# Softmax denominators by 32x32 transposes and one product, in a two-layer attention kernel on one core

## The chip, the core and the metric

The kernel runs on one core of a Trainium2 chip. The core has five engines that work side by side, each with an in-order queue of its own: TensorE (PE, matrix products; PEld in the profile is its weight load), VectorE (DVE), ScalarE (ACT), GpSimd (POOL) and SyncE (SP). SP and POOL, and at the start ACT, also issue DMAs. The metric is the device time of one execution in microseconds (us); several executions give a median.

## What is computed

Two self-attention layers follow each other on 4 images of 64x64 tokens with 256 channels, all in float32. Cut to what matters:

```python
# first layer, N = 4096 tokens, queries and keys of 32 channels, values of 256
q, k, v = x @ Wq + bq, x @ Wk + bk, x @ Wv + bv
x = gamma * softmax(q @ k.T) @ v + x
# second layer, values of 128 channels, then a product back to 256
f, g, v = x @ Wf + bf, x @ Wg + bg, x @ Wh + bh
x = x + (softmax(g @ f.T) @ v) @ Wo + bo
```

## The kernel before

The function `fast_path` holds all the work here. Scores are computed transposed, keys on partitions and queries along the free axis, so the exponentials feed the next product with no transpose. No maximum is subtracted; a check at the end looks whether all sums and values stayed in range, and otherwise a general path runs (it doesn't here).

**Blocks and steps.** An image takes 16 blocks of 256 queries in the first layer (8 steps each, 4 key tiles of 128 a step) and 8 blocks of 512 queries in the second (16 steps each, 2 key tiles a step). A `Step` computes scores `st` on PE, and ACT turns them into `p` (L544). Where a step is split, for precision, ACT also makes a rounded `high` (L542), DVE makes `low = p - high` (L555) and a correction `d` (L560), and PE multiplies all three with their own parts of the values. All first-layer steps are split, and steps 0, 3, 5, 8, 11 and 13 of a second-layer block (`SPLIT1`). Other second-layer steps multiply `p` itself, in full float32 (two records on PE for each product).

**Order.** The main loop runs over all steps. In step n it writes `d` of n, `low` of n+1, the addition to the sums, the scores of n+2, then side work, then the products of n. Side work comes from `plan`: projections of the coming layer or image (`transpose_unit`, `qk_unit`, `v_unit`) and the ends of the block before, each put at a step by number. A scheduler sets the final order on each engine from this.

**Denominators.** In the first layer a column of ones in the values gives them. In the second they are summed apart: over a block, `p` of most steps is added into `p_sum` on DVE (L571, L573), and `p` of the steps in `MOVED_SUMS` is added into `p_sum_moved` (slot `e`) by DMAs issued from POOL, the first as a copy (L548), the others accumulating (L550). `end_second` adds both (L659), takes `o` from the accumulators (L657), folds the two key tiles (L660, `sums`), and returns four `output` units, put at steps 1 to 4 of the next block. Each one multiplies 128 queries of `o` with `Wo` (L667), and, to sum over partitions and turn the result, multiplies the same 128 columns of `sums` with one column of ones:

```python
nc.tensor.matmul(ps[:, C : C + 1], sums[:, tok], ones[:, :1], start=True, stop=True)   # L668
nc.vector.reciprocal(inverse[:, 1, n : n + 1], ps[:, C : C + 1])                        # L670
y = small(f"y_{key}_{t}")
nc.scalar.activation(y, ps[:, :C], AF.Copy, scale=inverse[:, 1, n : n + 1])             # L673
```

POOL then adds `y` to the output in memory by an accumulating DMA (L675).

**Buffers.** `wide` tiles are 128x1024: slots `t` (2, for `high` and for `p` of split second-layer steps), `p` (3), `l` (2), `d` (1, `d` of the first layer and `p_sum`) and `e` (1). `small` tiles are 128x256 (4 slots): `x_res` and `x1` of the first layer's ends, `y`, and `good` of the final check. `whole` in `qk_unit` has a buffer of its own.

**Queues.** SP loads `x_res` (L750) and `squares` (32x32 pieces of the input that DVE transposes into `xT`, L392), and stores `x1`, the first part of the output, and queries and keys (L446). POOL loads queries and keys back (L493), adds biases (L639, L751), and issues the moved sums.

**End.** After the last output DVE checks `inverse` and `seen_v` (L808 to L819), PE counts (L821), and all engines read the flag.

Of the kernel before, what the change touches and what calls it, by code (L numbers as in the profile page):

```python
# [57 lines left out]
P = 128  # L58
# [9 lines left out]
SPLIT1 = (0, 3, 5, 8, 11, 13)  # L68
MOVED_SUMS = (0, 4, 7, 9, 12)

# [168 lines left out]
def fast_path(ctx: ExitStack, tc: tile.TileContext, x, w0, w1, wo, bo, gamma, out, off):  # L239
# [27 lines left out]
    def wide(tag, name, dtype=F32):  # L267
        return work.tile([P, 2 * QB], dtype, tag=tag, bufs={"d": 1, "e": 1, "p": 3}.get(tag, 2), name=name)

# [39 lines left out]
    nc.vector.memset(ones, 1.0)  # L309

    inverse = const.tile([P, 2, B * N // P], F32, name="inverse")
    seen_v = const.tile([P, 2, B * NH], F32, name="seen_v")
# [11 lines left out]
    for l, (q_w, q_b, k_w, k_b, v_w, v_b) in enumerate((w0, w1)):  # L324
        queue = (nc.scalar, nc.gpsimd)[l]
        w_sb = work.tile([P, NCC, 2 * D], F32, tag="small", bufs=4, name=f"wqk_whole{l}")
        b_sb = const.tile([2 * D, 1], F32, name=f"bqk{l}")
        for g, w_dram, b_dram in ((0, q_w, q_b), (D, k_w, k_b)):
            queue.dma_start(w_sb[:, :, g : g + D], w_dram.rearrange("(c p) d -> p c d", p=P))
            queue.dma_start(b_sb[g : g + D, :], b_dram.rearrange("(d o) -> d o", o=1))  # L330
        w_parts = const.tile([P, NCC, 4 * D], F32R, name=f"wqk{l}")
        high, low = w_parts[:, :, : 2 * D], w_parts[:, :, 2 * D :]
        nc.scalar.copy(high, w_sb)
        nc.vector.tensor_sub(low, w_sb, high.bitcast(F32))
        wqk.append(w_parts)
        bqk.append(b_sb)
        v_sb = const.tile([P, NCC, CV[l]], F32, name=f"wv{l}")
        queue.dma_start(v_sb, v_w.rearrange("(c p) d -> p c d", p=P))
        wv.append(v_sb)
# [20 lines left out]
    def bias_units():  # L360


        def issue():
            nc.vector.tensor_scalar(bv, bv, gamma_sb, None, ALU.mult)
            wide_bias = work.tile([P, P], F32, tag="small", bufs=4, name="wide_bias")
            nc.vector.memset(wide_bias, 1.0)
# [8 lines left out]
    qk_dram, x1_dram = {}, {}  # L375
    q_t, moved_sums, first_p, waiting = {}, {}, [], {}

# [34 lines left out]
    def project_units(b, l, h):  # L412
# [5 lines left out]
        def qk_unit():  # L418
            ps = side_psum(f"psqk_{b}_{l}_{h}")[:, :QB0]
            for c in range(NCC):  # L420
                for n in range(2):
# [6 lines left out]
                    )  # L428
            whole = data.tile([2 * D, QB0], F32, tag="qk", name=f"qk_{b}_{l}_{h}")
            lead = b == l == 0 and h % 2 == 1  # L430
# [16 lines left out]
            halves[b, l, j] = part + 1  # L447
            if l == 0 and b > 0:
                load_half(b, h + 1)
            elif l == 1 and h == NH - 1:  # L450
                load_half(b + 1, 0)
            elif l == 1:
                load_squares((b, 1, h + 1), waiting.pop((b, h + 1)))
            if b == l == 0:
# [36 lines left out]
    def load_rows(dst, parts, which, order):  # L491
        for n, h in enumerate(order):
            nc.gpsimd.dma_start(dst[n * D : (n + 1) * D, :], parts[h, which])  # L493

# [15 lines left out]
    def small(name):  # L510
        return work.tile([P, C], F32, tag="small", bufs=4, name=name)


    class Step:
# [8 lines left out]
        def scores(self):  # L523
# [16 lines left out]
            if self.split:  # L540
                self.high = wide("t", f"high_{self.key}", F32R)
                nc.scalar.activation(self.high, s_flat, AF.Exp, bias=down)  # L542
            self.p = wide("t" if self.split and l == 1 else "p", f"p_{self.key}")
            nc.scalar.activation(self.p, s_flat, AF.Exp)  # L544
            if l == 1 and i in MOVED_SUMS:
                if i == MOVED_SUMS[0]:
                    moved_sums[b, j] = wide("e", f"p_sum_moved_{b}_{j}")
                    nc.gpsimd.dma_start(moved_sums[b, j], self.p)  # L548
                else:
                    nc.gpsimd.dma_start(moved_sums[b, j], self.p, accum_op=ALU.add)  # L550
# [12 lines left out]

        def add_up(self, p_sum):
            if self.l == 0 or self.i in MOVED_SUMS:
                return
            kept = [i for i in range(NI[1]) if i not in MOVED_SUMS]
            if self.i == kept[0]:
                first_p.append(self.p)
            elif self.i == kept[1]:  # L570
                nc.vector.tensor_add(p_sum, first_p.pop(0), self.p)  # L571
            else:
                nc.vector.tensor_add(p_sum, p_sum, self.p)  # L573

# [78 lines left out]

    def end_second(b, j, acc, p_sum, o):
        key = f"{b}_{j}"
        for h in range(QB // QB0):
            nc.vector.tensor_add(o[h][:, :QB0], o[h][:, :QB0], acc[1][:, h * QB0 : (h + 1) * QB0])  # L657
        sums = work.tile([P, QB], F32, tag="sums", bufs=1, name=f"sums_{key}")
        nc.vector.tensor_add(p_sum, p_sum, moved_sums[b, j])  # L659
        nc.vector.tensor_add(sums, p_sum[:, :QB], p_sum[:, QB:])  # L660

        def output(t):
            def issue():
# [3 lines left out]
                nc.tensor.matmul(ps[:, :C], part, wo_sb, start=True, stop=True)  # L667
                nc.tensor.matmul(ps[:, C : C + 1], sums[:, tok], ones[:, :1], start=True, stop=True)  # L668
                n = (b * N + j * QB) // P + t
                nc.vector.reciprocal(inverse[:, 1, n : n + 1], ps[:, C : C + 1])  # L670

# [6 lines left out]

        return [output(t) for t in range(NT)]

    def run(units):
        for u in units:
            u()


# [13 lines left out]
    keys = [(b, l, j) for b in range(B) for l in range(2) for j in range(NB)][NB:]  # L699
    acc, p_sum, units = None, None, {}  # L700

    def plan(b, l, j, ends):
# [20 lines left out]
        else:  # L723
            for n, u in enumerate(ends):
                put(1 + n, u)
        if b + 1 < B:
            for h in range(NH):
# [7 lines left out]
    for n, s in enumerate(steps):  # L735
        b, l, j = s.b, s.l, s.j
        if s.first:
            units = plan(b, l, j, ends)
            acc = [ps_main.tile([P, QB], F32, tag=f"acc{a}", name=f"acc{a}_{b}_{l}_{j}") for a in range(2)]
            if l == 0:  # L740
                pair = ps_main.tile([P, 2, QB], F32, tag="pair", name=f"acc_pair_{b}_{j}")
                acc += [pair[:, a, :] for a in range(2)]
            if l == 1:
                p_sum = wide("d", f"p_sum_{b}_{j}")
        if l == 0 and s.last:
# [22 lines left out]
        after.cut_low()  # L768
        s.add_up(p_sum)
        todo = units.get(s.i, [])  # L770
# [30 lines left out]
        if s.last:  # L801
            ends = end_first(b, j, acc) if l == 0 else end_second(b, j, acc, p_sum, o)
    run(ends)

    good = small("good").rearrange("p (l n) -> p l n", l=2)
    nc.vector.tensor_scalar(good, inverse, 1.0 / SUM_MAX, None, ALU.is_ge)  # L808
    nc.vector.tensor_scalar(inverse, inverse, 1.0 / SUM_MIN, None, ALU.is_le)
    nc.vector.tensor_mul(good, good, inverse)  # L810
    nc.vector.tensor_scalar(seen_v, seen_v, VALUE_MAX, None, ALU.is_le)
    size = const.tile([P, 1], F32, name="size")
    nc.vector.tensor_mul(size, gamma_sb, gamma_sb)
    nc.vector.tensor_scalar(size, size, GAMMA_MAX**2, None, ALU.is_le)
    low = const.tile([P, 1], F32, name="low")
    for seen, axes in ((good, AX.XY), (seen_v, AX.XY)):
        nc.vector.tensor_reduce(low, seen, axes, ALU.min)
        nc.vector.tensor_mul(size, size, low)
    nc.vector.tensor_scalar(low, size, 1.0, None, ALU.is_lt)  # L819
# [53 lines left out]
```

## Time and profile before

| what | value |
|---|---|
| median of 3 runs | 3159.63 us (3158.0 to 3161.63) |
| profiled execution, its own time | 3155.92 us |
| span of the profiled execution | 3154.1 us |
| busy PE / DVE / ACT / POOL | 3116.3 / 2689.1 / 2140.1 / 900.7 us |
| accumulating DMAs of the moved sums, issue to landing | 4.5 / 4.9 / 6.5 us (least, median, most) |
| longest total wait on ACT | `high` for scores on PE, 362.8 us in 358 waits |

Busy time is the time in which an engine has an instruction running; matrix products are pipelined and their ends are modelled. In a row of groups stand line, engine, operation, output and inputs with shapes, the count, then busy time and mean duration in ns, then the idle time ahead of the group and what ended it. In a timeline the first two numbers are start and duration. Names without numbers stand for all buffers of that name.

### The profile page before, as it was taken

To read this page: it belongs to the slowest core of one execution; us is meant where nothing else is said; L and a number is where in the kernel's file an instruction comes from. 1 tells how busy PE (TensorE), PEld (TensorE's weight loads), DVE (VectorE), ACT (ScalarE), POOL (GpSimd) and SP (SyncE) were. 2 spreads that over 40 slices of the span, in tenths; PEclk is the share of its full clock that TensorE was granted. 3 is DMA by queue.
4 is the path that set the end of the run, shared out by engine and by line. 5 is a ranking of instruction groups with operands and counts; after the bars stand their busy time and mean duration, and the time that the engine had idled before them with its cause. 6 is when DMAs were issued, how large, how long until landed. Compare 5 with 4: busy or idle time off the path is not lost.

```text
span 3154.1 us, 54090 instructions
## 1 busy us (share of the span) xinstructions
PE 3116.3 (99%) x19908; PEld 2672.0 (85%) x19908; DVE 2689.1 (85%) x3237; ACT 2140.1 (68%) x2835; POOL 900.7 (29%) x1108
## 2 busy tenths in 40 slices
PE   8999999999999999999999999999999999999997
PEld 7999998666799999866679999976668999996664
DVE  7888888888888888888888888898888888888876
ACT  7666666777666666777766666677776666666674
POOL 5232224222422222422242222232223222233221
PEclk9999999999999999999999999999999999999999
DMA  4121114555512121555541112255554111125454
GB/s 119 43 53 47 48 48 104 107 108 105 104 44 51 41 53 47 113 101 112 107 93 47 49 45 51 51 116 107 105 113 81 48 46 47 49 65 105 97 95 73
DMA packets 391392, 239.49 MB, mean 76 GB/s; under 512 B 266672, under 2 KB 355248, under 8 KB 391120
## 3 DMA queue, kind: packets, MB, share of 16 engines
q0 software_dynamic: 68160, 134.86, 22.0%
q1 hardware_dynamic: 322048, 100.76, 13.4%
q8 instruction: 161, 2.64, 0.4%
q14 instruction: 111, 0.91, 0.1%
q10 hardware_dynamic: 912, 0.33, 0.1%
HBM read 82.58 MB, written 67.11 MB: 47 GB/s over the span
## 4 chain that ended last, share of the span: by engine, by line
PE 91%; DVE 3%; DMA 2%; issue 2%; ACT 1%; POOL 0%; SPq 0%; DVEq 0%; ACTq 0%; POOLq 0%
PE acc L600 24%; PE acc L582 23%; PE acc_pair L582 23%; PE st L532 14%; PE psv L464 4%; PE psqk L422 2%; PE pso L667 2%; DVE d L560 1%; DVE low L555 1%; ACT p L544 1%; DVE p_sum L573 1%; DMA p_sum_moved<-p 0%; DMA squares<-in_x 0%; PE pso L668 0%; DMA squares<-x_dram 0%
## 5 line engine op out<-in xcount | busy, mean ns | idle before, releaser
L542 ACT ACTIVATE high<-st,down 128x1024 fp32r<-128x1024 f32 x704 | 786.5, 1117 | 703.2 <-PE st L532 362.8
L544 ACT ACTIVATE p<-st 128x1024 f32<-128x1024 f32 x1024 | 1042.5, 1021 | 166.3 <-PE st L532 143.8
L560 DVE SCALAR_TENSOR_TENSOR d<-low,high 128x1024 fp32r<-128x1024 f32 x704 | 871.0, 1237 | 227.0 <-PE acc_pair L582 223.7
L555 DVE TENSOR_TENSOR low<-p,high 128x1024 fp32r<-128x1024 f32 x704 | 936.6, 1330 | 142.6 <-ACT p L544 141.6
L532 PE MATMUL st<-q,k 128*128 128x256 f32 (+1 forms) x3072 | 706.3, 338 | 2.5 <-DMA k<-qk_parts 1.4
L600 PE MATMUL acc<-p,v 128*128 128x512 f32 x1280 | 611.0, 597 | 0.0
L532 PEld LDWEIGHTS st<-q,k 128*128 128x128 f32 x3072 | 470.0, 189 | 103.3 <-issue 40.6
L639 POOL TENSOR_TENSOR x_res<-x,bo 128x256 f32<-128x256 f32 x128 | 212.5, 1660 | 879.3 <-DVE x L628 879.2
L600 PEld LDWEIGHTS acc<-p,v 128*128 128x128 f32 x1280 | 233.1, 189 | 161.8 <-issue 143.4
L573 DVE TENSOR_TENSOR p_sum<-p_sum,p 128x1024 f32<-128x1024 f32 x288 | 352.6, 1224 | 9.4 <-ACT p L544 5.8
L582 PE MATMUL acc<-v0h,high 128*128 128x258 f32 x2048 | 341.6, 284 | 1.2 <-ACT high L542 1.2
L582 PE MATMUL acc<-v0d,d 128*128 128x258 f32 x2048 | 339.2, 287 | 2.6 <-DVE d L560 2.2
L582 PE MATMUL acc<-v0l,low 128*128 128x256 f32 (+1 forms) x2048 | 329.3, 283 | 0.6 <-DVE low L555 0.5
L582 PE MATMUL acc_pair<-v0h,high 128*128 128x258 f32 x2048 | 329.8, 283 | 0.0
L582 PE MATMUL acc_pair<-v0l,low 128*128 128x256 f32 (+1 forms) x2048 | 328.8, 282 | 0.0
L582 PE MATMUL acc_pair<-v0d,d 128*128 128x258 f32 x2048 | 328.5, 282 | 0.0
L582 PEld LDWEIGHTS acc<-v0h,high 128*128 128x128 f32 x2048 | 286.0, 189 | 3.1 <-issue 1.4
L582 PEld LDWEIGHTS acc<-v0d,d 128*128 128x128 f32 x2048 | 281.5, 190 | 5.6 <-DVE d L560 4.9
L582 PEld LDWEIGHTS acc<-v0l,low 128*128 128x128 f32 x2048 | 282.2, 190 | 1.8 <-DVE low L555 1.3
L582 PEld LDWEIGHTS acc_pair<-v0h,high 128*128 128x128 f32 x2048 | 282.1, 189 | 0.0
L582 PEld LDWEIGHTS acc_pair<-v0l,low 128*128 128x128 f32 x2048 | 281.1, 189 | 0.0
L582 PEld LDWEIGHTS acc_pair<-v0d,d 128*128 128x128 f32 x2048 | 281.0, 189 | 0.0
(108 smaller groups left out, 3332.5 us busy)
## 6 DMA issues: line engine op xcount, KB each, us to landing
p_sum_moved<-p POOLq DMA_DIRECT2D x160, 512.0 KB, 4.7
x_res<-in_x SPq DMA_DIRECT2D x128, 128.0 KB, 2.1
qk_dram<-qk_parts SPq DMA_DIRECT2D x128, 128.0 KB, 1.9
x_dram<-x SPq DMA_DIRECT2D x128, 128.0 KB, 1.7
out<-x_res SPq DMA_DIRECT2D x128, 128.0 KB, 1.7
squares<-x_dram SPq DMA_DIRECT2D x512, 32.0 KB, 1.9
out<-y POOLq DMA_DIRECT2D x128, 128.0 KB, 3.2
q<-qk_dram POOLq DMA_DIRECT2D x252, 64.0 KB, 2.2
```

The costliest lines, as they stand in the source:

```text
L422: nc.tensor.matmul(ps, wqk[l][:, c, :], x_parts[key][n][:, c, :], start=(c == n == 0), stop=(c == NCC - 1 and n == 1),)
L464: nc.tensor.matmul(ps[:, t, :], xT[key][:, c, t * P : (t + 1) * P], wv[l][:, c, :], start=(c == 0), stop=(c == NCC - 1),)
L532: nc.tensor.matmul(st[:, g, :], k_t[b, l, kt // NT][:, kt % NT * P : (kt % NT + 1) * P], q_t[b, l, j * n // QB][:, q0 : q0 + n], start=Tru ...
L542: nc.scalar.activation(self.high, s_flat, AF.Exp, bias=down)
L544: nc.scalar.activation(self.p, s_flat, AF.Exp)
L555: nc.vector.tensor_sub(self.low, self.p, self.high.bitcast(F32))
L560: nc.vector.scalar_tensor_tensor(self.d, self.low.bitcast(F32), -UP, self.high.bitcast(F32), ALU.mult, ALU.add)
L573: nc.vector.tensor_add(p_sum, p_sum, self.p)
L582: nc.tensor.matmul(acc[2 * s + which][:, :width], p[:, g * QB0 + s * P : g * QB0 + (s + 1) * P], v0[self.i][v][:, g, :width], start=self.f ...
L600: nc.tensor.matmul(acc[which], v_part[:, g, :], p[:, g * QB : (g + 1) * QB], start=first and g == 0, stop=last and g == G[1] - 1,)
L639: nc.gpsimd.tensor_add(x_old[s], x_new[s], bo_sb)
L667: nc.tensor.matmul(ps[:, :C], part, wo_sb, start=True, stop=True)
```

## The change

It has five parts.

1. The denominators of all second-layer blocks but the very last are computed in two new units ahead of the outputs. `turn` transposes the 512 columns of `sums` in 32x32 squares on DVE and reduces each square, which leaves 16 partial sums on each partition. `denominators` multiplies those with a constant `same` (ones where two partitions have the same number modulo 32) on PE, and four reciprocals of 32 partitions each write `inverse`. The four outputs follow at steps 3 to 6. The last block keeps the column of ones.
2. Six steps instead of five are moved sums: 3, 4, 6, 7, 9, 12. The first is split, and ACT writes its `p` straight into slot `e`, so there is no copy; the other five accumulate into it. `issue_after` puts these DMAs behind the load of queries or keys that was written last. `p_sum` is allocated at the second kept step, and `sums` lies in its first half, the transposed squares in its second.
3. Slot `t` has three buffers, `small` three, and `whole` is a `small` tile.
4. In `qk_unit` the loads of the next half block's `squares` are written ahead of the store of queries and keys.
5. The check of all earlier blocks is put at step 13 of the last block, and only the last four columns are checked at the end. `good` is a `t` tile.

```diff
-MOVED_SUMS = (0, 4, 7, 9, 12)
+MOVED_SUMS = (3, 4, 6, 7, 9, 12)
...
-        return work.tile([P, 2 * QB], dtype, tag=tag, bufs={"d": 1, "e": 1, "p": 3}.get(tag, 2), name=name)
+        return work.tile([P, 2 * QB], dtype, tag=tag, bufs={"d": 1, "e": 1, "p": 3, "t": 3}.get(tag, 2), name=name)
...
+    same = const.tile([P, P], F32, name="same")
+    nc.gpsimd.tensor_copy(same[:, :S], ident[:, :S])
+    for a in range(1, P // S):
+        nc.gpsimd.tensor_add(same[:, :S], same[:, :S], ident[:, a * S : (a + 1) * S])
+    for a in range(1, P // S):
+        nc.gpsimd.tensor_copy(same[:, a * S : (a + 1) * S], same[:, :S])
...
+            if l == 0 and b > 0:
+                load_half(b, h + 1)
+            elif l == 1 and h == NH - 1:
+                load_half(b + 1, 0)
+            elif l == 1:
+                load_squares((b, 1, h + 1), waiting.pop((b, h + 1)))
-            whole = data.tile([2 * D, QB0], F32, tag="qk", name=f"qk_{b}_{l}_{h}")
+            whole = small(f"qk_{b}_{l}_{h}")[: 2 * D, :]
...
-            nc.gpsimd.dma_start(dst[n * D : (n + 1) * D, :], parts[h, which])
+            loads[0] = nc.gpsimd.dma_start(dst[n * D : (n + 1) * D, :], parts[h, which])
...
-        return work.tile([P, C], F32, tag="small", bufs=4, name=name)
+        return work.tile([P, C], F32, tag="small", bufs=3, name=name)
...
-            self.p = wide("t" if self.split and l == 1 else "p", f"p_{self.key}")
+            base = l == 1 and i == MOVED_SUMS[0]
+            self.p = wide("e" if base else "t" if self.split and l == 1 else "p", f"p_{self.key}")
             nc.scalar.activation(self.p, s_flat, AF.Exp)
-            if l == 1 and i in MOVED_SUMS:
-                if i == MOVED_SUMS[0]:
-                    moved_sums[b, j] = wide("e", f"p_sum_moved_{b}_{j}")
-                    nc.gpsimd.dma_start(moved_sums[b, j], self.p)
-                else:
+            if base:
+                moved_sums[b, j] = self.p
+            elif l == 1 and i in MOVED_SUMS:
+                with tc.issue_after(loads[0].ins):
                     nc.gpsimd.dma_start(moved_sums[b, j], self.p, accum_op=ALU.add)
...
-        sums = work.tile([P, QB], F32, tag="sums", bufs=1, name=f"sums_{key}")
-        nc.vector.tensor_add(p_sum, p_sum, moved_sums[b, j])
-        nc.vector.tensor_add(sums, p_sum[:, :QB], p_sum[:, QB:])
+        sums, squares = p_sum[:, :QB], p_sum[:, QB:]
+        nc.vector.tensor_add(sums, sums, squares)
+        n0 = (b * N + j * QB) // P
+        end = b == B - 1 and j == NQ[1] - 1
+        part_sums = work.tile([P, QB // S], F32, tag="part_sums", bufs=1, name=f"part_sums_{key}")
+
+        def turn():
+            nc.vector.transpose(squares, sums)
+            nc.vector.tensor_reduce(part_sums, squares.rearrange("p (n k) -> p n k", k=S), AX.X, ALU.add)
+
+        def denominators():
+            ps = side_psum(f"psd_{key}")[:, : QB // S]
+            nc.tensor.matmul(ps, same, part_sums, start=True, stop=True)
+            for a in range(P // S):
+                rows = slice(a * S, (a + 1) * S)
+                of_rows = ps[rows, :].rearrange("p (t a) -> p t a", a=P // S)[:, :, a]
+                nc.vector.reciprocal(inverse[rows, 1, n0 : n0 + NT], of_rows)
...
-                nc.tensor.matmul(ps[:, C : C + 1], sums[:, tok], ones[:, :1], start=True, stop=True)
-                n = (b * N + j * QB) // P + t
-                nc.vector.reciprocal(inverse[:, 1, n : n + 1], ps[:, C : C + 1])
+                n = n0 + t
+                if end:
+                    nc.tensor.matmul(ps[:, C : C + 1], sums[:, tok], ones[:, :1], start=True, stop=True)
+                    nc.vector.reciprocal(inverse[:, 1, n : n + 1], ps[:, C : C + 1])
...
-        return [output(t) for t in range(NT)]
+        return ([] if end else [turn, denominators]) + [output(t) for t in range(NT)]
...
+        if (b, j) == (B - 1, NQ[1] - 1):
+            put(NI[1] - 3, check_all_but_last)
...
     run(ends)
-    good = small("good").rearrange("p (l n) -> p l n", l=2)
...
+    check(in_last_block)
```

## The prediction

> **What bounds the kernel now.** I read the page first, then busy time by stretches, then the timeline of single edges.
>
> ```profile
> PE 3116.3 (99%) x19908; PEld 2672.0 (85%) x19908; DVE 2689.1 (85%) x3237; ACT 2140.1 (68%) x2835; POOL 900.7 (29%) x1108
> ...
> PE 91%; DVE 3%; DMA 2%; issue 2%; ACT 1%; POOL 0%; SPq 0%; DVEq 0%; ACTq 0%; POOLq 0%
> ```
>
> TensorE (PE) holds the chain. A busy PE could still hide waits in modelled ends, so the next table asks where it is idle (columns: length, then busy time and count of PE, PEld, DVE, ACT, POOL, clock, DMA).
>
> ```profile
> core 0: us, PE busy (x) PEld busy (x) DVE busy (x) ACT busy (x) POOL busy (x), PEclk, DMA share, GB/s
> 0.00:80.00 80.00, 66.75 (x390) 56.74 (x391) 56.63 (x139) 56.49 (x115) 41.48 (x86) 1.00 0.46 119
> 80.00:160.00 80.00, 77.21 (x606) 74.34 (x605) 66.96 (x85) 51.65 (x68) 17.21 (x22) 1.00 0.17 43
> ...
> 2875.00:3134.00 259.00, 258.74 (x899) 164.59 (x897) 206.52 (x218) 174.85 (x202) 67.24 (x91) 1.00 0.50 95
> 3134.00:3154.20 20.20, 3.20 (x19) 2.59 (x18) 4.80 (x17) 1.79 (x4) 3.55 (x4) 0.70 0.24 30
> ```
>
> Of 37.8 us of idle PE (3154.1 - 3116.3), 13.3 + 2.8 lie in the first 160 us and 17.0 after 3134. About 5 us are left for the rest. So in the body an edit pays only by taking work off PE, and costs only where it makes PE wait. Buffers and earlier loads have next to nothing to win there.
>
> **What the Trainium skill says.** "TensorE: Matmul & The Clock Gate", section LDWEIGHTS, prices a weight load at its columns over 1.2 ns, 107 ns for 128; a wide product hides it, a one-column product can't. The trace agrees: a product L668 comes as two records, some 0.23 us together (below), near two bare loads. "VectorE: DVE Perf Modes", section The three transpose paths: the DVE transposes 32x32 blocks and never crosses them, which is why one product with `same` must still join the four groups of partitions; the trace has that transpose at 0.705 us. "Perfetto Trace Analysis", section Identifying the Most-Contended Engine: matmul busy share is no measure of headroom, and consistent bubbles mean missing buffers. Here the steps are regular and the bubbles absent. "DMA: Bandwidth & Descriptors", section Two DMAs through the same engine are not ordered: a dependent DMA needs the earlier one's semaphore. The trace shows POOL waiting so, 45.2 us in 13 waits of L550 for the last accumulation.
>
> **Part 1, the denominators.** Before, each of 128 outputs has a product L668. In the PE timeline:
>
> ```profile
> 2240.28 0.28 PE L668 MATMUL pso<-ones,sums 128*128 128x1 f32 x2
> 2240.42 1.96 PE L600 MATMUL acc<-p,v 128*128 128x512 f32 x4
> 2241.82 1.02 PE L532 MATMUL st<-q,k 128*128 128x512 f32 x2
> ...
> 2257.82 1.88 PE L600 MATMUL acc<-p,v 128*128 128x512 f32 x4
> 2259.13 1.03 PE L600 MATMUL acc<-d,v 128*128 128x512 f32 x2
> ```
>
> First column is the start. L668 holds PE for 0.14 us, and the group behind it then takes 1.40 us to the next start, against 1.31 without L668 ahead: 0.23 us each. 31 of 32 blocks change (the last keeps the old way): 124 x 0.23 = 28.5 us removed. Added: 31 products of 16 columns, two records each, same loads; 15 more columns are estimated at 0.01 us, so 31 x 0.24 = 7.4 us. **Net -21.1 us on PE.** All of it is on the path.
>
> VectorE (DVE), durations by form:
>
> ```profile
> L573 DVE TENSOR_TENSOR p_sum<-p_sum,p 128x1024 f32<-128x1024 f32 x288 | 352.6, 1224 | 9.4 <-ACT p L544 5.8
> L392 DVE STREAM_TRANSPOSE xT<-squares 128x512 f32<-128x512 f32 x112 | 79.0, 705 | 15.2 <-DMA squares<-in_x 6.5 <-DMA squares<-x_dram 5.1 <-issue 3.0
> L670 DVE RECIPROCAL inverse<-pso 128x1 f32<-128x1 f32 x128 | 20.5, 162 | 15.2 <-PE pso L668 14.2
> L817 DVE TENSOR_REDUCE low<-good 128x1 f32<-128x256 f32 x1 | 0.4, 420 | 0.0
> ```
>
> Removed: one 1.22 us addition per block, since six sums move instead of five. Added: a transpose of 0.70, and a reduction over 512 that I estimate at 0.69 from the 256-wide one (0.42) and the 512-wide passes (0.68 to 0.70). Four reciprocals stay four. Per block +0.17 us, 5 us over the run, under PE's work.
>
> **New waits in part 1.** The product with `same` waits for transpose and reduction. In the built order it stands behind the second whole step's product of the next block. Worked out from the edge at 2994: d done 2995.9, transpose to 2996.5, low (behind its p) to 2998.0, reduction to 2998.7; PE arrives at 2998.5. Where the reduction stands ahead of low, as in the last image, there is no wait. So 0 to 0.2 us. Queued behind it on PE are the next score product and the first output; behind the reciprocals on DVE the next d; ACT's y waits for the inverses, with all later exponentials behind it. ACT is 68% busy, which covers a wait of half a us.
>
> The second wait is for d. These lines of one edge show the cover that goes:
>
> ```profile
> 2994.57 0.59 PE L667 MATMUL pso<-wo,o 128*128 128x256 f32 x2
> 2994.66 1.22 DVE L560 SCALAR_TENSOR_TENSOR d<-low,high 128x1024 fp32r<-128x1024 f32 x1
> ...
> 2995.00 0.28 PE L668 MATMUL pso<-ones,sums 128*128 128x1 f32 x2
> 2995.14 1.96 PE L600 MATMUL acc<-p,v 128*128 128x512 f32 x4
> ...
> 2996.54 1.04 PE L600 MATMUL acc<-d,v 128*128 128x512 f32 x2
> ```
>
> d ends at 2995.88, PE takes it at 2996.54: 0.66 us to spare, just what L667 and L668 (0.43 + 0.23) occupy ahead of it. The outputs now start two steps later, so PE comes 0.66 us sooner. Edges of the first image spare 0.34 to 0.78 us in the same count, so 0 to 0.3 us is lost per edge. Both waits together: 0 to +8 us over 31 edges. I take **+3**.
>
> **Part 2, moved sums.** The copy L548 goes; p of step 3 is written straight into the slot `e`, and steps 4, 6, 7, 9, 12 accumulate. DMA count stays 160, but five of a block now queue one behind another, 4.9 us each (median of L550; 4.5 to 6.5). In the last image p of step 4 is issued 28.1 us ahead of L659, so five take 24.5 and the last lands some 3.5 us ahead (before: 3.6 to 5.5). Covered: 0. Behind these waits on POOL stand the stores of y and the next q loads. `issue_after` keeps the k and q loads ahead. DMA time may also fall or rise with accumulation in place of copy; I bound this part at -2 to +4 and take 0.
>
> **Part 3, buffers and queues.** The third `t` lets high of step 3 start when its scores are done, 1.2 us sooner at the edge above (it waited 1.58 us). PE was not waiting for it: 0, bounds -3 to 0. `small` has three slots and takes `whole` as well. Two x_res, two x1 and one `whole` share them in the first layer; SP's order now loads x_res behind the store of q and k, and x1 of the second tile comes 3.3 us after the first, whose store lands in 1.7 and whose POOL addition takes 1.7. In the second layer, y of one tile may wait for an earlier store (3.2 us). ACT would stop, not yet PE: 0 to +3, taken as 0. Loads of squares ahead of the store of queries and keys: eight DMAs move past one on SP; DVE's waits for them are 11.6 us in all, PE's share is within the 5 us above. -2 to +1, taken 0.
>
> **Part 4, start and end.** Seven small POOL instructions for `same` go between its weight loads. The nearest row is the POOL memset of 128x128, 0.20 us, so each load is 0.2 to 1.5 us later, and the ACT cast of the second layer's weights and DVE's gamma step wait for them in their queues. Against that, x_res leaves SP's first loads. -1 to +3, taken **+1**. The end:
>
> ```profile
> 3138.70 0.47 ACT L673 ACTIVATE y<-pso,inverse 128x256 f32<-128x256 f32 x1 [0.18 <-DVE inverse L670]
> 3140.65 0.29 DVE L808 TENSOR_SCALAR good<-inverse 128x256 f32<-128x256 f32 x1 [1.99 <-DMA out<-y]
> ...
> 3143.30 0.19 PE L821 MATMUL count<-low,ones 128*1 128x1 f32 x2 [4.85 <-DVE low L819]
> ```
>
> `good` waits 2.0 us for a slot of `small` that a store of y holds; it moves to `t`, and eight instructions shrink to six of four columns (2.5 to 1.2 us). POOL's last store is issued until 3140.8 and then bounds it: -2.9. The early checks sit between the last additions and push the last sums back by some 0.6. Hence -2.3, say **-2** (0 to -3.5).
>
> **Sum.** -21.1 + 3 + 1 - 2 = -19 us, 0.6%. The profiled execution took 3155.9 us around a span of 3154.1, and would give 3137. The median of the three runs lies 3.7 us above that, at 3159.6; I forecast **3140.5**.
>
> **Rivals.** *New waits take most of it.* If each of 31 edges loses 0.5 us at d and at the inverses, 15.5 instead of 3: -6.6 us, 3153. For it: the exact match of spare time and removed cover. Against: other products stand there in blocks with projections. *The chain of moved sums becomes the bound* (slower). If landings take 6.4 us, as two did in the last image, five need 32 us, 4 us beyond the add; 1.4 us of that may be covered, and in some 13 blocks with 35 us between adds 2.7 us are lost, +35 us: 3176. It decides from a mean landing of 5.6 us; the median of 4.9 speaks against it. *The edit does not do what it says*: PE hides L668 in part, say 0.14 us each. Then 17 - 5 = 12 is gained, with the other terms 3149. The longer group behind L668 speaks against it.
>
> **Chances.** Forecast 0.66, edges 0.13, partial price 0.10, chain 0.11. A measurement of this kernel tells about 0.2%, 6.3 us. Faster: forecast, partial price and a little of the edge case, 0.78; same 0.11; slower 0.11. Range 3132 (all low bounds but a few) to 3155 (the edge case).
>
> **What would show it.** L668 falls to 8 records, and the new product has 62 records, PE busy near 3095. Right waits: PE idle in the body still some 5 us; more than 15 would be the edge rival. The chain rival shows as the final p_sum addition waiting for a DMA. The prediction is wrong if PE busy falls by under 12 us, or if idle grows by as much as it falls.

## The result and the profile after

The changed kernel takes 3203.5 us (median of 4, 3198.1 to 3204.7) against 3158.8 us before (4, 3156.4 to 3161.6) in the same session. The ratio is 1.0138, 95% interval 1.012 to 1.0155: 44 us slower, where 19 us faster were forecast. Below, the effect of a run is its ratio to before, less one, times 3158.8 us.

Busy times and the chain of waits by engine, after:

```profile
PE 3123.4 (98%) x19722; PEld 2656.5 (83%) x19722; DVE 2710.0 (85%) x3272; ACT 2136.8 (67%) x2835; POOL 855.0 (27%) x1115
...
PE 74%; DVE 9%; DMA 6%; issue 6%; SPq 2%; ACT 1%; POOL 1%; DVEq 0%; ACTq 0%; POOLq 0%
```

PE has 186 records fewer, as the change says, yet its busy time rose by 7.1 us, and its share of the chain fell from 91% to 74%. DVE and DMA took the place. Busy time by stretches (columns as in the prediction's table) shows that it isn't the start:

```profile
core 0: us, PE busy (x) PEld busy (x) DVE busy (x) ACT busy (x) POOL busy (x), PEclk, DMA share, GB/s
160.00:500.00 340.00, 335.38 (x2774) 332.88 (x2772) 288.15 (x332) 219.86 (x281) 72.87 (x74) 1.00 0.19 47
500.00:900.00 400.00, 392.47 (x1754) 281.47 (x1753) 349.57 (x424) 280.65 (x387) 127.10 (x182) 1.00 0.56 105
```

The same stretches kept PE busy for 339.94 and 399.16 us before. The first of them is first layer only, which holds no denominators and no moved sums: 4.6 us of new idle time come from parts that were priced at nothing.

Since ends on PE are modelled, idle time understates this. So I priced each product at its usual distance to the next start (0.12 us for 256 or 258 columns, 0.23 for 512, 0.43 for 512 in full float32, 0.11 for a record of a one-column product) and counted what is left of each gap over 0.04 us. By this estimate PE's work falls by **20.8 us, near the forecast (21.1)**; since a record has one price in the whole count, this confirms how many records went, not what one is worth (e9 below does that). The gaps grow from some 51 to some 117 us, **about 66 us more**; with a usual distance for each pair of neighbouring products it is 70. The largest group of them stands ahead of the products that take `d`. Groups by line after; behind the bar stand busy time and mean, behind the second bar the idle time ahead of the group and what ended most of it:

```profile
L594 PE MATMUL acc<-v0d,d 128*128 128x258 f32 x2048 | 355.5, 291 | 27.0 <-DVE d L571 25.9
L594 PEld LDWEIGHTS acc<-v0d,d 128*128 128x128 f32 x2048 | 285.6, 190 | 45.0 <-DVE d L571 43.1
```

Before, these two idled 2.6 and 5.6 us. One first-layer edge after (where a block ends and the next begins), from the timeline (start, duration):

```profile
412.18 2.94 POOL L807 TENSOR_TENSOR x_res<-x_res,bv 128x256 f32<-128x256 f32 x2 [3.53 <-ACT high L551]
...
412.77 1.75 DVE L566 TENSOR_TENSOR low<-p,high 128x1024 fp32r<-128x1024 f32 x1
...
414.44 1.23 DVE L414 TENSOR_TENSOR xl<-xT,xh 128x512 fp32r<-128x512 f32 x1
...
416.12 1.21 DVE L571 SCALAR_TENSOR_TENSOR d<-low,high 128x1024 fp32r<-128x1024 f32 x1
...
417.38 0.63 PE L594 MATMUL acc<-v0d,d 128*128 128x258 f32 x3 [0.92 <-DVE d L571]
```

Two additions of `bv` on POOL (L751 before) run just while DVE has `low`, `xl`, both `o` and `d` to do with no gap. `low` takes 1.75 us instead of 1.22 and `xl` 1.23 instead of 0.69: 1.07 us lost, and PE waits 0.92 us for the `d` at the end of that queue. After has 42 waits of over 0.3 us ahead of these products, 33 us in sum. In the 7 us ahead of 41 of them DVE instructions were lengthened beside an addition of `bv`, by 31 us in sum. Before has four such waits, none of them with such an addition ahead. At the same edge before:

```profile
417.06 1.76 DVE L555 TENSOR_TENSOR low<-p,high 128x1024 fp32r<-128x1024 f32 x1
...
417.70 1.72 POOL L751 TENSOR_TENSOR x_res<-x_res,bv 128x256 f32<-128x256 f32 x1
```

POOL slowed `low` there too, but behind the edge (`x` was done at 412.6 and 415.9), where PE was not waiting. This addition is for the next block: before, an addition stands 22.7 us (median) ahead of the `x` that uses it, just behind the last edge; after, 7.6 us ahead, inside its own edge. Over the whole run `low` and `d` exceed 1.22 us by some 91 us in sum before and some 100 us after (counting excesses over 0.1 us, additions of both biases together). The amount of contention grows little; what changes most is its place. The Trainium skill, page "SBUF — State Buffer", section Who interferes with whom, describes this neighbour: a DVE instruction with two SBUF inputs contends with a GpSimd instruction that reads SBUF, over a port pair that they share. The trace agrees in kind: no `low`, `d` or `xl` is lengthened by over 0.1 us without a POOL addition beside it. A `low` that is hit mostly takes some 0.48 to 0.58 us longer (137 of 150 before).

### The profile page after: what moved, and what is told of

The parts are those of the page before. It is cut to its first block, busy times and chain, and to the rows that moved or that the text cites. A ratio compares the mean times of both kernels' runs of the same rounds, so it can differ in the third digit from the quotient of the medians.

```text
span 3201.7 us, 54037 instructions
## 1 busy us (share of the span) xinstructions
PE 3123.4 (98%) x19722; PEld 2656.5 (83%) x19722; DVE 2710.0 (85%) x3272; ACT 2136.8 (67%) x2835; POOL 855.0 (27%) x1115
## 4 chain that ended last, share of the span: by engine, by line
PE 74%; DVE 9%; DMA 6%; issue 6%; SPq 2%; ACT 1%; POOL 1%; DVEq 0%; ACTq 0%; POOLq 0%
PE acc L612 20%; PE acc_pair L594 18%; PE acc L594 17%; PE st L541 12%; PE psv L473 4%; DVE d L571 4%; DVE low L566 2%; PE psqk L430 2%; DMA x_res<-in_x 2%; DMA p<-p 2%; PE pso L697 1%; SPq L280 1%; DMA squares<-x_dram 1%; DVE xl L414 1%; DVE p_sum L585 1%
## 5 line engine op out<-in xcount | busy, mean ns | idle before, releaser
L571 DVE SCALAR_TENSOR_TENSOR d<-low,high 128x1024 fp32r<-128x1024 f32 x704 | 890.3, 1265 | 266.1 <-PE acc_pair L594 258.7
L566 DVE TENSOR_TENSOR low<-p,high 128x1024 fp32r<-128x1024 f32 x704 | 926.8, 1317 | 109.1 <-ACT p L555 107.8
L594 PE MATMUL acc<-v0d,d 128*128 128x258 f32 x2048 | 355.5, 291 | 27.0 <-DVE d L571 25.9
L585 DVE TENSOR_TENSOR p_sum<-p_sum,p 128x1024 f32<-128x1024 f32 x256 | 312.1, 1219 | 19.4 <-ACT p L555 17.0
L561 POOL DMA_DIRECT2D p<-p x160 | 143.4, 896 | 643.5 <-ACT p L555 289.0
L651 POOL TENSOR_TENSOR x_res<-x,bo 128x256 f32<-128x256 f32 x128 | 178.7, 1396 | 475.5 <-DVE x L640 306.7
```

The costliest lines, as they stand in the source:

```text
L566: nc.vector.tensor_sub(self.low, self.p, self.high.bitcast(F32))
L571: nc.vector.scalar_tensor_tensor(self.d, self.low.bitcast(F32), -UP, self.high.bitcast(F32), ALU.mult, ALU.add)
L585: nc.vector.tensor_add(p_sums[self.b, self.j], so_far, self.p)
L594: nc.tensor.matmul(acc[2 * s + which][:, :width], p[:, g * QB0 + s * P : g * QB0 + (s + 1) * P], v0[self.i][v][:, g, :width], start=self.f ...
L651: nc.gpsimd.tensor_add(x_old[s], x_new[s], bo_sb)
```

## The experiments

**Which part loses.** e4 undoes the prediction's part 3, e5 makes part 1 alone, e6 parts 2 and 4 alone.

```diff
 e4 (on after)
-... bufs={"d": 1, "e": 1, "p": 3, "t": 3}
+... bufs={"d": 1, "e": 1, "p": 3}
-            whole = small(f"qk_{b}_{l}_{h}")[: 2 * D, :]
+            whole = data.tile([2 * D, QB0], F32, tag="qk", name=f"qk_{b}_{l}_{h}")
-tag="small", bufs=3
+tag="small", bufs=4
 # and the load_half / load_squares lines back behind the store
 e5 (on before): `same` and the new end_second (`sums` in p_sum, the final p_sum addition ahead of `o`)
 e6 (on e4): the old end_second
```

> The kernel after with the whole third part undone: two high buffers, four slots in `small`, the sums in their own tile, the squares loads behind the store of queries and keys. What is left is the denominators, the moved sums and the check spread out. Theory A: 3158.8 - 21 (PE work removed) + 2 to 5 (edge waits) = 3138 to 3145 us. Rival B: the same. Rival C: still 3190 to 3205, the loss is in what is left.

e4: 1.0048 (1.0031 to 1.0065), +15 us. The gaps of the first image's first layer are nearly gone (under 0.7 us in each 79 us, some 1.5 to 3 after), but it does not reach 3140. Theory A explains only a part.

> The kernel before with the new end of a second-layer block alone (32x32 transposes, one product for all denominators, p_sum added to before o); the moved set, the buffers and the order of loads are those of before. e4 showed that without the third part the change still loses 17 us although 21 us of PE work are gone. Theory E (the new moved set is at fault: steps 1 and 2 of each second-layer block now put two p_sum additions of 1.22 us on DVE ahead of x of the last first-layer block, so x_dram, the squares, xT and the last keys come late, and at the other edges low and p come late): 3160 - 21 + 2 to 5 = 3141 to 3145 us. Theory C (the denominators' chain at the edge is at fault): 3165 to 3180.

e5: 1.0004 (0.9995 to 1.0012), +1 us: neither theory. The 21 us are saved and given back.

> e4 with the old end of a second-layer block, 124 sums products on PE again, so that the moved sums (3, 4, 6, 7, 9, 12), the base written straight into its tile, and the check spread out are what is left of the change. Theory E: the 17 us of e4 plus the 21 us of PE work, less 2 to 5 for the edge waits: 3193 to 3200 us. Theory C: 3155 to 3163, as before.

e6: 1.0056 (1.0039 to 1.0073), +18 us, where E had wanted twice that. So part 2 loses 14 us (e4 less e5) to 18 us whether part 1 is there or not, and part 1 is worth nothing either way.

**Buffers and queues.** e1 and e2 undo one or two of the three buffer changes, e3 and e15 make one or two alone, e8 undoes the order of loads, e11 leaves out POOL's additions.

```diff
 e2 (on after): "t": 3 taken out
 e1 (on e2)
-            whole = small(f"qk_{b}_{l}_{h}")[: 2 * D, :]
+            whole = data.tile([2 * D, QB0], F32, tag="qk", name=f"qk_{b}_{l}_{h}")
 e15 (on before): tag="small", bufs=4 becomes 3
 e3 (on e15)
-            whole = data.tile([2 * D, QB0], F32, tag="qk", name=f"qk_{b}_{l}_{h}")
+            whole = small(f"qk_{b}_{l}_{h}")[: 2 * D, :]
 e8 (on after): the load_half / load_squares lines behind the store
 e11 (on after)
-                nc.gpsimd.tensor_add(x_res[b, j][t], x_res[b, j][t], bv)
```

> The kernel after, with the query and key sums (`whole`) back in a tile of their own, tag qk; `small` stays at three slots, and the high tiles have two buffers again, which makes the room. Theory A (the sums in the ring of `small` put the x_res loads behind the store of queries and keys, so the bv additions on POOL run beside the busiest stretch of DVE at the block's edge, d is late, and PE waits about 1 us in each first-layer block): the loads stand again right behind the output stores, stalls on acc<-v0d,d fall from 52 us to under 20, time 3140 to 3160 us. Rival B (the squares loads ahead of the store do it): still 3195 to 3205, since that order stays. Rival C (moved sums and denominators at the edges): still 3195 to 3205. Rival D (third high buffer lets ACT run ahead of DVE): about 3140 to 3160 too, told apart by e2.

> The kernel after with two buffers for the high tiles, and nothing else undone. Theory A: no change against after, 3195 to 3210 us. Rival D (the third buffer is the harm): 3140 to 3160. If the third buffer helped after a little, as its purpose would have it: some us above after.

e1: 1.0103 (1.0087 to 1.012), +32 us; e2: 1.0206 (1.0189 to 1.0223), +65 us. The `small` tiles form a ring: they take its slots in turn, and a new one has to wait until the last user of its slot is done. The place of `whole`, the query and key sums, in this ring alone is worth 33 us here. In e1 the additions stand 22.1 us ahead of `x` again, and the gaps ahead of the first layer's `d` products fall from 52 to 16 us, as A said. Its time stays far above A's, in the range of B and C: it keeps three slots (e15 below) and the moved sums (e4). e2 also shows what was not forecast: the third `t` **gains** 22 us (65 less 43.6). With two, ACT's `high` waits 233.6 us for DVE's `low`; with three, `low` is no longer among the main releasers of its row.

> The kernel before with only this changed: `small` has three slots and the query and key sums take one of them. Theory A: the loss without the gain: 3158.8 + 40 to 65 = 3199 to 3224 us, with acc<-v0d,d waiting for DVE as in after. Rivals B, C and D: no change, 3155 to 3163.

> The kernel before with `small` at three slots, and nothing else. e3 lost 57 us with three slots and the sums of queries and keys in one of them. Theory A as refined (the ring's order does it, the slot does little): 3160 to 3175 us. If the missing slot is what costs: 3195 to 3220.

e3: 1.0174 (1.0157 to 1.0191), +55 us. e15: 1.0056 (1.0041 to 1.0072), +18 us. The suspected cost alone, in the kernel before, is larger than the whole loss of the change; two thirds of it, 37 us, are the sums in the ring. With them there the additions stand 7.4 us ahead of `x` in e3, as in after; with three slots alone 19.9 us. So the slot costs in another place: see the table under "Moved sums".

> The kernel after with one thing undone: the squares loads stand again behind the store of queries and keys. Theory A: nothing comes back, 3195 to 3212 us, since the x_res loads stay behind both. Rival B (the order of squares and store is at fault for part of it): 3180 or less.

e8: 1.0168 (1.0151 to 1.0185), +53 us, 9 above after, with intervals that just touch. The earlier loads seem to help a little; rival B falls.

> The kernel after without the addition of bv to x_res on POOL (128 instructions of about 1.4 us); the second layer gets an input without it. The loads of x_res stay late. Theory A (the additions beside DVE's busiest stretch make d late): the 52 us of stalls on acc<-v0d,d fall under 20, 3160 to 3175 us. If the late loads do the harm in another way (x late, the order of DVE): 3190 to 3205 us.

e11: 1.0006 (0.9997 to 1.0014), +2 us. **Leaving out 128 small POOL instructions, with every load as late as in after, gives back 42 us.** Groups by line of e11:

```profile
L594 PEld LDWEIGHTS acc<-v0d,d 128*128 128x128 f32 x2048 | 285.7, 190 | 10.9 <-DVE d L571 7.3
```

45.0 became 10.9. A rival would be that the additions hold up other work in POOL's queue while they wait for their loads. But the gaps of PE fall by 39 us, and 37 of these stand ahead of the products that take `d`, where the lengthened DVE instructions were seen. A load stands 12.0 us (median) ahead of its `x` in e11, 12.9 in after, 25.4 before: the lateness does no harm by itself; where POOL then runs does. No run leaves the additions out of the kernel before; there PE waits for `d` ahead of these products for only 2.2 us on its own row, so little could come back at this place.

**Moved sums.** e7 takes the early additions off DVE, e12 moves one more step in e5.

```diff
 e7 (on e4, add_up): steps 0 to 2 are not added, step 5 twice
+            if self.i <= 2:
+                return
+            so_far = self.p if self.i == kept[3] else p_sums[self.b, self.j]
 e12 (on e5)
-MOVED_SUMS = (0, 4, 7, 9, 12)
+MOVED_SUMS = (0, 1, 4, 7, 9, 12)
```

> e4 with the sums of steps 0, 1 and 2 left out (step 5 is counted twice in their place), which takes the two p_sum additions of steps 1 and 2 away from DVE in each of the 32 second-layer blocks; the five accumulating DMAs and their order on POOL stay. Theory E: the stalls at the edges of the second layer go back to a few us, 3143 to 3155 us. If the accumulating DMAs, or the order that holds them behind the loads of keys, are at fault: still 3172 to 3182.

e7: 0.997 (0.9959 to 0.9982), -10 us, 25 below e4. DVE has 78 us less to do in it (64 x 1.22), so this is an upper bound for what the two additions cost in their place. POOL, which waits for landings of the moved sums for 137.2 us in after and 45.2 before, keeps its five DMAs in e7, so they are not what costs the 25 us. What the additions hold up is seen in e4's timeline where the first layer ends:

```profile
523.53 1.22 DVE L585 TENSOR_TENSOR p_sum<-p,p 128x1024 f32<-128x1024 f32 x1
...
524.86 1.23 DVE L585 TENSOR_TENSOR p_sum<-p_sum,p 128x1024 f32<-128x1024 f32 x1
...
527.56 0.87 DVE L640 SCALAR_TENSOR_TENSOR x<-o,g,x_res 128x256 f32<-128x256 f32 x2
528.06 0.81 SPq L644 DMA_DIRECT2D x_dram<-x  x2
...
532.98 0.33 SPq L280 DMA_DIRECT2D squares<-x_dram  x1
```

Before, with step 0 moved, the first addition came behind the first `x`:

```profile
524.74 0.49 DVE L628 SCALAR_TENSOR_TENSOR x<-o,g,x_res 128x256 f32<-128x256 f32 x1
525.23 1.23 DVE L571 TENSOR_TENSOR p_sum<-p,p 128x1024 f32<-128x1024 f32 x1
```

So `x` is 2.8 us later, the store too, and `squares` 3.1 us later (529.91 before). PE then waits until 555.6 us for keys that POOL loaded late, 1.0 us, and shorter for `xh`, `xl` and `p` around it. All four images show the same. In the table, an edge is the last first-layer product of an image; the second column is the time from there to the first load of `squares` from the new `x`, the third how long PE idles from 20 us before to 80 us after, four images together:

| run | `squares` after the edge | PE idle at four edges |
|---|---|---|
| before | 8.2 to 8.5 us | 1.3 us |
| e5 (denominators alone) | 8.2 to 8.5 us | 2.4 us |
| e4 (all but part 3) | 12.0 to 12.8 us | 15.1 us |
| e6 (moved sums alone) | 11.9 to 12.3 us | 13.3 us |
| e7 (e4 without the early sums) | 7.2 to 7.5 us | 5.7 us |
| e15 (three slots alone) | 11.0 us | 10.7 us |

This is where e4 and e6 lose, and e7 gets most of it back. By the count of gaps, all of the 24 us that e4 has more than e5 stand at these edges, and 17 of the 19 us that e15 has more than before. The missing slot of e15 costs at the same edge by another way: its second `x` comes 3.6 us behind the first (1.7 before), and `squares` is loaded behind both.

> e5 with step 1 added to the moved set of before: (0, 1, 4, 7, 9, 12), with the copy into the moved tile as before. One p_sum addition fewer (1.22 us of DVE) in each second-layer block, at its start, where e7 showed such additions to cost most. Theory E: e5 less 5 to 12 us, 3151 to 3158 us. If one more accumulating DMA early in the block holds up the loads of keys behind it on POOL: 3165 to 3180 us.

e12: 1.0011 (1.0003 to 1.002), +3 us, nothing gained over e5. E's forecast fails here. `squares` comes 7.3 to 7.7 us after the edge in e12, but e5 has no loss at this edge to win back (2.4 us): a late `x` costs, and one that is earlier than before gains nothing.

**Denominators.** e9 takes the old products away, and e13, e17 and e16 put pieces of the new way in.

```diff
 e9 (on before)
-                nc.tensor.matmul(ps[:, C : C + 1], sums[:, tok], ones[:, :1], start=True, stop=True)
-                nc.vector.reciprocal(inverse[:, 1, n : n + 1], ps[:, C : C + 1])
+                nc.vector.reciprocal(inverse[:, 1, n : n + 1], sums[:, t : t + 1])
 e13 (on e9):  return [nothing, nothing] + [output(t) for t in range(NT)]
 e17 (on e13): return [turn, nothing] + [output(t) for t in range(NT)]
 e16 (on e5), in turn
-            nc.vector.transpose(squares, sums)
-            nc.vector.tensor_reduce(part_sums, ..., AX.X, ALU.add)
+            nc.vector.tensor_copy(part_sums, sums[:, : QB // S])
 e10 (on e5): turn empty, part_sums = sums[:, : QB // S]
 e14 (on e5): denominators and the first output in one unit
```

> The kernel before with the 128 one-column products (line 668) left out; the reciprocals stay, of a column of `sums` instead, so that DVE does what it did and the y are scaled wrongly. It gives what the price of these products is worth when nothing is put in their place. e5 gained nothing, although its PE work is 21 us less. Theory F (in the steps where these products stand PE is held to the pace of DVE and ACT anyway, and what it saves it waits): 3153 to 3163 us. Theory G (the saving is real, and the transposes, the reduction and the wait for the product eat it): 3161 - 29 = 3132 to 3137 us.

> e5 without the transposes and the reduction (0.7 and 0.64 us of DVE in each of 31 edges): the product takes the first 16 columns of the sums instead, so the denominators are wrong. Theory G (the added work of DVE at the edge eats the saving): 3163 less 15 to 20, 3140 to 3148 us. Theory F: 3155 to 3163, no change against e5.

e9: 0.9921 (0.9907 to 0.9934), -25 us: of the 29 us that 128 products are worth by the forecast's price, most come through. (The reciprocals no longer wait for PE either, so not all of it need be PE's time.) F falls. e10: 1.0001 (0.9993 to 1.001). It says nothing of G, since the product reads `p_sum` there and the next `p_sum` waits for it, 13 us on DVE; what e13's expectation takes from e10 does not hold.

> e9 (the kernel before without the 128 sums products, with reciprocals of a column of `sums`) with two empty units ahead of the four outputs, so that these stand at steps 3 to 6 of the next block as in the change, and no transposes, no product for the denominators. e10 showed that the transposes and the reduction are not what eats the 24 us that e9 gained. Theory H (the two units ahead move the outputs by two steps: ACT's y and PE's pso then stand at steps that already carry high and p of the split steps 3 and 5 and the projections of the next image, p and st come late): 3152 to 3162 us. Theory J (the one product, its wait and its place in the side PSUM ring cost it): 3133 to 3139, as e9.

> e13 (no sums products, outputs two steps later, 3139 us) with the transposes and the reduction on DVE at step 1, whose result nobody reads. Theory G: 3139 plus 12 to 20, 3151 to 3159 us. Theory J: 3137 to 3143 us.

> e5 with the transposes and the reduction left out, and a DVE copy of the first 16 columns of the sums into part_sums in their place, so that the denominators are wrong. e10 did the same but let the product read p_sum itself, so that the next p_sum had to wait for PE (13 us on DVE in its trace); the copy takes that wait away. Theory G (the 1.3 us of DVE at each edge eat the saving): 3163 less 12 to 20, 3143 to 3150 us. Theory J (the product, its four reciprocals and their waits do): 3157 to 3165.

> e5 with the denominators and the first output in one unit: turn at step 1, product and first output at step 2, the others at 3 to 5. Correct values. Theory H: about half of the loss comes back, 3148 to 3156 us. Theory J: 3158 to 3166, as e5, or more, since the first y now waits for the reciprocals.

e13: 0.9941 (0.9927 to 0.9955), -19 us. e17: 0.9958 (0.9945 to 0.9972), -13 us. e16: 0.9975 (0.9965 to 0.9984), -8 us. e14: 1.0007 (0.9999 to 1.0015), +2 us. None of the theories holds alone: e13 and e14 fall in J's ranges, e16 in G's, e17 between the two. Going from e9 to e5, 26 us are lost. `turn` takes 9 us of them where the product follows (e5 less e16); that is clear of the intervals. Smaller steps are not: some 6 us for the later outputs (e13 less e9) and some 5 us for `turn` without the product (e17 less e13) have intervals that overlap. The rest, 11 to 15 us, is the product (an estimated 7.4 us of its own time on PE) together with all else by which e5 differs from e13 and e17: the four reciprocals and their waits, `sums` inside p_sum, and the final p_sum addition ahead of `o`. No run parts these. One wait on the way shows in the groups by line of e5:

```profile
L680 PEld LDWEIGHTS psd<-part_sums,same 128*128 128x128 f32 x62 | 10.6, 188 | 14.6 <-DVE part_sums L675 11.0 <-issue 3.1
L680 PE MATMUL psd<-part_sums,same 128*128 128x16 f32 x62 | 9.9, 236 | 2.0 <-DVE part_sums L675 1.8
```

and of e16:

```profile
L679 PEld LDWEIGHTS psd<-part_sums,same 128*128 128x128 f32 x62 | 11.5, 188 | 2.5
```

The loads of the product idle 14.6 us, 11.0 of it until the reduction, and 2.5 us when a copy of 0.17 us stands in its place. But a load can idle while an earlier product still runs, and PE's own row idles only 2.0 us there (2.6 by the count of gaps). So this wait is a small part of the 9 us. By the count of gaps most of the difference is spread over other products: ahead of the scores 22 us in e5 against 16 in e16, of the outputs 10 against 5, of `low` 8 against 4.

**A version made of what helped.** e18 is e5 with the third `t`, the earlier loads, three `small` slots, and the sums in a tile of their own.

```diff
 e18 (on e5): "t": 3, tag="small" bufs=3, load_half / load_squares ahead of the store
-            parts = data.tile([P, QB0], F32R, tag="v1_parts" if lead else "qk_parts", ...)
+            parts = x_parts[key][1][:, 1, :]
```

> A version with right values that keeps what the runs showed to help and leaves what they showed to cost: the denominators of e5 with the moved set of before, the third high buffer (e2: worth 24 us in the kernel after) and the squares loads ahead of the store (e8: 10 us), while the sums of queries and keys have a tile of their own; the room comes from their parts, which lie in the low half of x, read by then, and from three slots in `small` (e15: costs 15 us). If the worths add up: 3163 - 24 - 10 + 15 = 3144 us, range 3135 to 3160, faster than both. If they were worth something only in the kernel after, where ACT and SP were late for other reasons: 3165 to 3180.

e18: 1.002 (1.0013 to 1.0027), +6 us. That is between the two ranges. The worths don't add up: third buffer and earlier loads repay some 13 of the 18 us that the missing slot costs, not 31 (the new place of the parts was not run alone). The second `x` still comes 3.7 us behind the first, and PE idles 12.4 us at the four edges. No version with the whole computation beat the kernel before.

**The account.** Along one path, each number with all changes up to there: before 0, denominators +1 (e5), moved sums and check +15 (e4), three slots with the loads ahead +32 (e1), sums in the ring +65 (e2), third `t` +44 (after).

## Why the prediction was wrong

- **Part 1, price on PE: right.** -21.1 was forecast, and the records went as counted. e9 gains 25 us (21 to 29) where the price says 29: PE's time at this place is worth about its price when nothing takes its place.
- **Part 1, new waits: +3 (0 to +8) failed.** They measure about 22 us (e5 at +1 instead of -21). The two waits that were priced are not where most of it went: PE's row waits 2.0 us for the product behind the reduction in all 31 edges, so "0 to 0.2 us" an edge was near, and the gaps ahead of products that take `d` grow by some 5 us. What had no price is the 1.3 us that `turn` puts on DVE at each edge, worth 9 us with the product behind it (the forecast set it off against a saved p_sum addition, as lying "under PE's work"), and the two steps' delay of the outputs, used only for the cover of `d` (some 6 us, not clear of noise). The other 7 us or so stay open: some 4 are missing in e9 already, the rest lies with the product, its reciprocals or the order of the final additions. The rival "new waits take most of it" came nearer in size, but its waits at `d` are not the ones seen.
- **Part 2: 0 (-2 to +4) failed, by the step that was not looked at.** I followed the DMAs. Their chain was covered as argued: the final addition L669 waits for nothing, and a landing takes 4.8 us, so the slower rival is refuted. The loss of 14 to 18 us is at the edge where the second layer starts, in what the new set leaves on DVE: steps 0 to 2 are all kept, their two additions stand ahead of `x` in its queue, and `squares` comes some 4 us later. The per-block DVE balance (+0.17 us) hid that.
- **Part 3: `small` 0 to +3, "ACT would stop, not yet PE", failed most.** It measures 55 us alone (e3). I saw that the loads would come behind the store of q and k, and asked who waits for the loads. The right question was what the additions behind them run beside when they start later: 37 of the 55 us. I also saw that the second x1 comes 3.3 us after the first, and took it as free; with three slots it is 3.6 us, `squares` waits for it, and this edge is where the other 18 us show. The third `t`, taken as 0, gains 22 us in the changed kernel; the loads of squares, taken as 0, about 9.
- **Part 4: +1 and -2, small.** The 21st `p` of ACT starts 0.7 us earlier than before, and from the last main product to the end it takes 21.6 us instead of 20.7: the gain at the check went to `y`, which with three slots waits for a store:

```profile
3187.60 0.47 ACT L704 ACTIVATE y<-pso,inverse 128x256 f32<-128x256 f32 x1 [1.96 <-DMA out<-y]
```

- **The frame failed with them.** "Buffers and earlier loads have next to nothing to win there" was read from 5 us of idle PE. It tells how little there is to win, and nothing of how much can be lost: with PE at 99%, DVE, at 85% over the run, had no gap in the edge shown, so a delay there came through. Of the stated signs, 8 records of L668 and 62 of the product came true; PE busy near 3095 did not (3123.4), and idle time rose by 40 us.

## What to carry to other kernels

Before a buffer's tag or count is changed, follow the tile's next loader and every engine whose work moves with it, and look at what runs beside that work in its new place, above all DVE beside POOL. When steps change sides between engines, look at the order in the queue at the busiest edge; a balance per block doesn't show it. A saving on the bounding engine is worth its price only if the new way adds no wait on an engine that is nearly as full.

## What was not expected of the hardware

The 128x1024 `low` mostly took some 0.54 us longer when it was hit beside a 128x256 POOL addition (1.22 to 1.75), and so did `xl` (0.69 to 1.23). `d`, which also has two inputs in SBUF, was hit less: of 187 that overlapped an addition before, 62 took over 0.1 us longer, most of these by less than 0.4; two additions beside one `d` cost it up to 1.3 us after. The addition itself takes from 0.73 to 1.83 us. And busy time on PE can grow (7.1 us) while its work shrinks (some 21 us).
